# Conditioned residual block, 16 x 512 tokens: the hand-listed order of head, window and last group is listed anew

## The chip, the cores and the metric

The kernel runs on one core of one Trainium2 chip. Time is device time of one launch in microseconds (us). A core has five engines with an instruction queue each: PE (TensorE, matrix products into PSUM), DVE (VectorE), ACT (ScalarE), POOL (GpSimd) and SP (SyncE, which here only issues transfers). Each engine takes its instructions strictly in order; between engines only semaphores hold. PSUM has eight banks of 128 x 512 f32; PE writes there, DVE and ACT read it, POOL works on SBUF alone.

## The reference

For every token (row x of 512 numbers) six branches are made, weighted, joined to 3072 numbers and sent through a two-layer network with a layer norm; the result is added to x.

```python
h = _ln(x, pw_g[pathway_ids], pw_b[pathway_ids])
h = _ln(h, cp_g[compartment_ids], cp_b[compartment_ids])
t = _ln(x, tm_g[time_steps], tm_b[time_steps])
m = x + _mlp_ln(memory_state, ...)[:, None, :]     # n, r alike
s = _ln(x, ms_g[scale_type], ms_b[scale_type])
cat = jnp.concatenate([w[0] * h, w[1] * t, w[2] * m, w[3] * n, w[4] * r, w[5] * s], axis=-1)
return x + _mlp_ln(cat, int_W1, int_b1, int_W2, int_b2, int_g, int_be)
```

There are 16 x 512 = 8192 tokens, `_mlp_ln` is silu between two products and a layer norm behind them, and everything is f32.

## The kernel before, in words

Tokens are sorted by their (compartment, scale type) group and taken in 16 windows of 512, a window being four blocks of 128 rows. The first layer is computed from three operands, each turned so that its 512 columns lie on partitions: X (x itself, for the branches m, n, r), V (x normed, for t and s) and H (the twice normed branch h). V has weights of its own for each block of 128, built on the spot by `s_part` and `build`.

All work is cut into small pieces with two-letter names, and three texts list them: ORDER (line 20: set-up, windows 0 and 1, the start of 2), WINDOW (line 53) and LAST (line 69, the last window). `run` (line 1213) goes through such a text and calls each piece's function, which records its instructions. Nothing is reordered afterwards: every engine gets its instructions in the order of the list, and the waits follow from the data. WINDOW is run for windows 0 to 14 and leaves out what has been done already. In a name such as `rd.c.1.4` the letter is the window in relation to the current one: `o` two before, `p` one before, `c` the current one, `n` the next, `m` the one after; the digits are blocks or pairs of blocks.

Windows 2 to 14 compute the X and H share of layer 1 with seven products of half blocks instead of eight, for each of two pairs p of blocks. That is where GpSimd's sums come in. The pieces that matter here:

| pieces | engine | what they do |
|---|---|---|
| `p7.w.p.k`, `vp.w.g.n` | PE | one half-block product of X and H (L407), of V (L416): 22 in a window |
| `l2.w.j` | PE | layer 2 of one block (L351) |
| `rd.w.p.i` | DVE | adds one half bank of PSUM to the SBUF tile `add` (L427): 22 in a window |
| `la` | DVE | reads layer 2 from PSUM, adds a row (L458) |
| `tv`, `tx`, `th`, `tz` | DVE | 32 x 32 transposes of V, X, H and of the hidden layer (L186) |
| `f1`, `f2`, `bd`, `lb` | DVE | work on two or three SBUF operands: pathway affine (L288, L289), compartment (L312), the four chunks of `build` (L231), the last norm (L484, L485) |
| `hv`, `xe`, `xm`, `lv` | DVE | small statistics |
| `ss.w.p.0` to `ss.w.p.3` | POOL | the four sums of X and H blocks for the seven products (L377, L381, L383, L385) |
| `sh.w.j` | POOL | adds a row to the x block (L320) |
| `wq`, `wr` | POOL | sums of the weights, before the first and after the last of these windows (L353 to L366) |
| `gx`, `gh`, `gc`, `ga`, `po` | POOL | gathers of x, pathway rows, compartment rows and layer-1 rows (L160), the scatter of the result (L489) |
| `xp`, `fp`, `lp` | POOL | inverse roots (L253, L304, L476) |
| `xs`, `hb`, `nv`, `xn`, `fn`, `sp`, `hs`, `lq` | ACT | sums, norms, the first half of the V weights (L225), silu, squares |
| `sX`, `sV`, `sH`, `sZ` | SP | the transfers that complete a transposition (L194) |

What can hold a POOL sum is data alone: `ss.w.p.0` needs the X rows landed, `ss.w.p.1` the H rows, `ss.w.p.2` and `ss.w.p.3` the end of the products that read the old values; `sh` needs only that the window's norms have been read. The seven products accumulate within a bank, so that a product can wait for a read (`rd`) of what stands there, and a read for a product.

Of the kernel before, what the change touches and what calls it, by code (L numbers as in the profile page):

```python
# [18 lines left out]

ORDER = """  # L20
    sz scl bx lt ax wk.1.3 h2.1 wk.1.0 ac lw wk.1.1 se xt.0.0 by h2.2 pwi dk lh sp.0.0 gh.0.1 gh.0.0 xt.0.1 kd
    bd.0.0 cv he.1 xv.0.1 xv.0.0 dp px tt gh.0.2 xs.0.0 wk.1.2 wk.2.3 tk xs.0.1 h2.0 pk xs.0.2 gx.e0.2 xs.0.3 eh.1
    wk.2.0 he.2 cg xe.0 he.0 gx.e0.1 wh xp.0 xt.0.2 eh.0 gx.e0.0 xm.0 dc wk.2.1 xn.0.0 eh.2 cs xt.0.3 nv.0.0 cp
    xv.0.3 wk.2.2 cn gc.0.0 tb tv.0.0 xv.0.2 ct gx.e0.3 lo xs.e0.2 xa xn.0.1 do xs.e0.0 gr.e0.0 ca lX.0.2 xs.e0.1
    f1.0.0 nv.0.1 nv.0.3 cm xs.e0.3 nv.0.2 gr.e0.2 hb.0.0 f1.0.1 xe.e0 gx.e1.3 tv.0.3 gx.e1.0 wm tv.0.2 tv.0.1
    lX.0.3 gx.e1.1 cr xp.e0 gc.0.1 xm.e0 nv.e0.0 sV.0.2 nv.e0.2 f2.0.0 xn.0.2 hb.0.1 mt.e0.0 nv.e0.3 nv.e0.1 tr.e0.0
    sV.0.3 sV.0.0 mt.e0.2 gx.e1.2 tr.e0.2 lX.0.0 f2.0.1 lX.0.1 gr.e0.3 sp.0.1 gr.e0.1 hv.0.1 xs.e1.2 mt.e0.3 gx.1.1
    gr.e1.1 fp.0.1 sV.0.1 gc.0.2 tr.e0.3 mt.e0.1 xs.e1.1 rp.1 tr.e0.1 gr.e1.3 gc.0.3 fn.0.1 bd.0.1 sE.e0.1 sE.e0.0
    xs.e1.3 xs.e1.0 f1.0.2 gh.0.3 xn.0.3 lV.0.0 gx.1.2 hb.0.2 rp.0 hv.0.0 sE.e0.2 lV.0.1 th.0.1 rc.0 xe.e1 f1.0.3
    f2.0.2 xp.e1 fp.0.0 hv.0.2 xm.e1 hb.0.3 gx.1.0 hv.0.3 gc.1.0 fp.0.2 rc.1 tx.1.1 ex.1 fn.0.0 fp.0.3 ex.0 sE.e0.3  # L30
    f2.0.3 nv.e1.1 fn.0.3 th.0.0 tx.1.0 ro.0 fn.0.2 gx.1.3 th.0.3 gh.1.3 sp.0.2 xs.1.3 xs.1.0 ro.1 nv.e1.0 th.0.2
    xs.1.2 sH.0.0 bd.0.2 xs.1.1 mt.e1.1 tr.e1.1 sH.0.2 ex.2 ea.0 ex.3 sp.0.3 tx.1.3 gr.e1.0 ee.0 gx.2.1 mt.e1.0
    tr.e1.0 gc.1.3 nv.e1.3 lV.0.2 eo.0 tx.1.2 xe.1 xp.1 nv.e1.2 gr.e1.2 gh.1.0 bd.0.3 ea.1 sh.0.2 xm.1 lH.0.0 ea.2
    gx.2.3 xs.2.1 mt.e1.2 nv.1.0 sH.0.1 lH.0.2 mt.e1.3 sX.1.1 xn.1.0 gh.1.2 lH.0.1 xn.1.3 ea.3 tr.e1.2 tr.e1.3 ea.4
    tv.1.0 sX.1.0 f1.1.3 sh.0.1 gx.2.0 gx.2.2 lV.0.3 xn.1.2 gc.2.0 f1.1.0 gc.1.2 ee.1 ee.2 hb.1.3 hv.1.3 sE.e1.0
    hb.1.0 lX.1.0 f2.1.3 nv.1.1 f1.1.2 ex.4 f2.1.0 sE.e1.1 wl.1 ex.5 ea.6 sH.0.3 eo.2 fp.1.3 sE.e1.2 nv.1.2 lH.0.3
    sp.1.1 ea.5 hv.1.0 fp.1.0 ee.3 nv.1.3 sh.0.3 ee.4 hb.1.2 ex.6 bd.1.1 xs.2.3 fn.1.0 gh.1.1 gc.1.1 ar eo.3 fn.1.3
    tv.1.1 wl.3 tv.1.3 f2.1.2 hv.1.2 th.1.0 fp.1.2 eo.4 tv.1.2 xn.1.1 gh.2.1 xs.2.0 sX.1.2 xs.2.2 ee.5 th.1.3 sX.1.3
    eo.1 wl.2 ee.6 eo.5 xe.2 f1.1.1 eo.6 xp.2 tx.2.0 sp.1.0 lX.1.2 lX.1.3 sh.1.2 fn.1.2 xm.2 hb.1.1 tx.2.3 tx.2.1
    bd.1.0 ga.0.0 ha.0.0 nv.2.2 sV.1.0 ga.0.2 hv.1.1 ga.0.3 f2.1.1 fp.1.1 wl.0 ha.0.2 sh.1.0 th.1.2 hs.0.0 ga.0.1  # L40
    fn.1.1 sh.1.3 th.1.1 hs.0.2 xn.2.1 f1.2.1 gc.2.1 wl.4 sh.1.1 gh.2.3 lX.1.1 lV.1.0 sp.1.2 sV.1.2 sh.0.0 ha.0.3
    hs.0.3 bd.1.2 sV.1.1 ha.0.1 lV.1.1 ga.1.2 sp.1.3 tx.2.2 xn.2.0 sV.1.3 gh.2.0 sH.1.0 tz.0.0 tv.2.2 ga.1.0 hs.0.1
    tz.0.2 wq.3 hb.2.1 sH.1.3 tz.0.1 lV.1.2 nv.2.1 bd.1.3 tz.0.3 wq.1 lH.1.0 lV.1.3 lH.1.3 f2.2.1 nv.2.0 sp.2.1
    tv.2.0 nv.2.3 sp.2.0 bd.2.1 ga.1.3 bd.2.0 f1.2.0 wq.2 xn.2.3 sH.1.2 sX.2.1 sH.1.1 hv.2.1 sZ.0.3 hb.2.0 fp.2.1
    tv.2.3 wq.0 ha.1.0 tv.2.1 fn.2.1 f2.2.0 hv.2.0 l2.0.3 sZ.0.1 sh.2.3 fp.2.0 ga.2.2 la.0.3 ha.1.3 l2.0.1 sZ.0.2
    la.0.1 sX.2.2 ga.2.0 lq.0.1 l2.0.2 hs.1.0 fn.2.0 sZ.0.0 sV.2.1 l2.0.0 sV.2.2 hs.1.3 ga.1.1 tz.1.0 sX.2.0 xn.2.2
    sV.2.0 la.0.2 lq.0.2 th.2.0 tz.1.3 la.0.0 lq.0.0 th.2.1 lq.0.3 lH.1.2 lv.0 lH.1.1 ha.1.2 sV.2.3 gh.2.2 hs.1.2
    lp.0 sX.2.3 gh.3.1 lb.0.1 lb.0.0 gx.3.1 gx.3.0 ha.1.1 po.0.1 hs.1.1 lb.0.3 gx.3.3 tz.1.2 xs.3.1 tz.1.1 ga.2.3
    po.0.0 lb.0.2 gx.3.2 xs.3.0 ga.2.1 po.0.2
"""  # L50
# [1236 lines left out]
```

## Time and profile before

| | us |
|---|---|
| three timed runs, median (lowest, highest) | 1129.79 (1126.06, 1133.42) |
| the profiled execution, as timed | 1131.24 |
| its span in the profile | 1129.5 |
| the head, up to the first product of window 2 | 210.1 |
| windows 2 to 14, from one first product to the next | 62.3 to 65.0 |
| the last group, from the last first product | 974.4 to 1129.5 |

The mean clock that TensorE was granted is 0.95. In the profile's lines an engine's name stands ahead of the line of the kernel (L231) and the operation; then come output and input by the program's names, the shape, and how many. Busy time of an engine is what its instructions took; idle time before an instruction is put down to what released it. POOL's share of DMA instructions is the time of their issue, not of the transfer.

The costliest groups of DVE and POOL that the change reorders, in the same execution:

| group | instructions | mean ns |
|---|---|---|
| L231 `build` | 252 | 952 |
| L289, second half of `f1` | 64 | 1213 |
| L312 `f2` | 64 | 1113 |
| L484, first half of `lb` | 56 | 1250 |
| L485, second half of `lb` | 56 | 897 |
| L186, transposes of H | 64 | 680 |
| L458 `la` | 64 | 671 |
| L377, L381, L383, L385 `ss` | 26 each | 1279, 1354, 1282, 1463 |

### The profile page before, as it was taken

How to read it: one execution, taken by the hardware profiler on the slowest of the kernel's cores; microseconds unless marked ns; L12 is line 12 of the kernel's file. 1: busy time of each engine (PE TensorE's matmuls, PEld its weight loads, DVE VectorE, ACT ScalarE, POOL GpSimd, SP SyncE). 2: the span in 40 equal slices, each digit the busy share in tenths (PEclk: the TensorE clock that was granted, in tenths of full speed). 3: DMA queues.
4: the chain of work that ended last, by engine and by line, in shares of the span. 5: the costliest groups of instructions: out<-in, count | busy, mean ns of one | idle time of the engine just before them, and what ended most of it. 6: DMA issues, size and time to landing. Idle time of an engine off the chain costs nothing. (4 is left out here: it accounts for less than half of the span.)

```text
span 1129.5 us, 13393 instructions
## 1 busy us (share of the span) xinstructions
PE 986.7 (87%) x3577; PEld 652.2 (58%) x3577; DVE 920.4 (81%) x1466; ACT 656.2 (58%) x1432; POOL 712.8 (63%) x702
## 2 busy tenths in 40 slices
...
GB/s 296 238 155 222 248 214 177 220 126 191 169 144 176 142 222 127 200 122 190 168 145 201 128 212 132 187 129 180 180 140 187 143 214 130 192 126 136 112 51 93
DMA packets 91895, 191.07 MB, mean 169 GB/s; under 512 B 25364, under 2 KB 25364, under 8 KB 91820
## 3 DMA queue, kind: packets, MB, share of 16 engines
...
q14 instruction: 46, 0.38, 0.1%
...
## 5 line engine op out<-in xcount | busy, mean ns | idle before, releaser
L351 PE MATMUL p<-w,cZ 128*128 128x512 f32 x512 | 225.9, 595 | 10.1 <-DMA cZ<-rZ 7.1
L231 DVE SCALAR_TENSOR_TENSOR vs<-wt,sct,vs 128x512 f32<-128x512 f32 x252 | 225.1, 952 | 0.0
L225 ACT ACTIVATE vs<-ws,scs 128x512 f32<-128x512 f32 x252 | 160.8, 708 | 23.6 <-PE pqv L416 21.2
L351 PEld LDWEIGHTS p<-w,cZ 128*128 128x128 f32 x512 | 95.4, 190 | 133.6 <-issue 132.0
L489 POOL DMA_INDIRECT out<-yb,tok x64 | 69.2, 1082 | 106.8 <-DVE yb L454 39.3
L294 ACT ACTIVATE junk<-pw 128x512 bf16<-128x512 f32 x64 | 40.2, 629 | 162.8 <-issue 100.9
L160 POOL DMA_INDIRECT pw<-in_pw,i_pw x64 | 63.9, 999 | 83.0 <-issue 51.1
L339 ACT ACTIVATE add<-add 128x512 f32<-128x512 f32 x64 | 38.9, 626 | 120.1 <-DVE add L427 79.6
L416 PE MATMUL pqv<-vs,cV 128*128 128x256 f32 x416 | 107.5, 398 | 0.4 <-DVE vs L231 0.4
L160 POOL DMA_INDIRECT xbs<-in_x,tok x64 | 71.2, 1113 | 51.3 <-DVE yb L485 30.8
L312 DVE SCALAR_TENSOR_TENSOR pw<-pw,mvh,cp 128x512 f32<-128x512 f32 x64 | 71.2, 1113 | 27.0 <-DMA cp<-cp_rows,i_cp 26.4
L416 PEld LDWEIGHTS pqv<-vs,cV 128*128 128x128 f32 x416 | 81.4, 200 | 19.6 <-DVE vs L231 7.9
L320 POOL TENSOR_TENSOR xbs<-xbs,rows 128x512 f32<-128x512 f32 x64 | 81.3, 1271 | 0.4
L160 POOL DMA_INDIRECT cp<-cp_rows,i_cp x64 | 66.5, 1039 | 22.9 <-issue 10.4
L160 POOL DMA_INDIRECT add<-rows,i_add x64 | 62.9, 983 | 26.6 <-issue 14.5
L289 DVE TENSOR_TENSOR pw<-pw 128x512 f32<-128x512 f32 x64 | 77.6, 1213 | 2.2
L308 ACT ACTIVATE pw<-pw,rsh 128x512 f32<-128x512 f32 x64 | 44.0, 711 | 51.5 <-DVE pw L312 45.1
L484 DVE SCALAR_TENSOR_TENSOR yb<-yb,rsy,rows 128x512 f32<-128x512 f32 x56 | 70.0, 1250 | 1.0 <-POOL rsy L476 1.0
L243 ACT ACTIVATE junk<-xbs 128x512 bf16<-128x512 f32 x72 | 44.8, 623 | 33.3 <-DMA xbs<-in_x,tok 31.9
L407 PE MATMUL pq_0b<-wh__80,cH 128*128 128x256 f32 x104 | 35.4, 500 | 27.8 <-DVE add L427 16.1
L381 POOL TENSOR_TENSOR cX<-cX,cH 128x512 f32<-128x512 f32 x26 | 35.2, 1354 | 36.3 <-DMA cH<-rH 33.6
L463 ACT ACTIVATE junk<-yb 128x512 bf16<-128x512 f32 x64 | 40.3, 630 | 28.2 <-DVE yb L458 26.4
...
## 6 DMA issues: line engine op xcount, KB each, us to landing
cV<-rV SPq DMA_DIRECT2D x256, 64.0 KB
cH<-rH SPq DMA_DIRECT2D x256, 64.0 KB
cZ<-rZ SPq DMA_DIRECT2D x256, 64.0 KB
...
```

The lines of the kernel that those rows point to most:

```text
L160: nc.gpsimd.indirect_dma_start(dst, None, table, bass.IndirectOffsetOnAxis(ap=idx, axis=0), **kw)
L225: nc.scalar.activation(v[:, c], ws[:, c], AF.Identity, scale=scs[:, c, g, w : w + 1])
L231: nc.vector.scalar_tensor_tensor(v[:, c], wt[:, c], sct[:, c, g, w : w + 1], v[:, c], ALU.mult, ALU.add)
L243: nc.scalar.activation(junk, x, AF.Identity, accum_out=sums[:, 0, j : j + 1])
L289: nc.vector.tensor_add(pw[:, :D], pw[:, :D], pw[:, D:])
L308: nc.scalar.mul(pw[:, :D], pw[:, :D], st.pop(("rs", j)))
L312: nc.vector.scalar_tensor_tensor(pw[:, :D], pw[:, :D], st["mv", j][:, 1:2], cp, ALU.add, ALU.mult)
L320: nc.gpsimd.tensor_add(st["xb"][:, j, :], st["xb"][:, j, :], rows[:, 2, :])
L351: nc.tensor.matmul(p2, st["cZ"][:, j, c, :], w2[:, c, :], start=(c == 0), stop=(c == NC - 1))
L416: nc.tensor.matmul(home, st["cV"][:, g, c], st["v", g][:, c, n * H : (n + 1) * H], start=(b == 0 and n == 1 and c == 0), stop=(c == NC - 1 ...
L484: nc.vector.scalar_tensor_tensor(y, y, st["rsy"][:, j : j + 1], rows[:, 1, :], ALU.mult, ALU.mult)
L489: nc.gpsimd.indirect_dma_start(out_rows, bass.IndirectOffsetOnAxis(ap=tok[:, j, w : w + 1], axis=0), yb[:, j, :], None)
```

## The change

The three lists hold the same pieces as before in another order. No function changes, no piece is added or left out, no size or buffer changes. What moves in WINDOW, beside many smaller things: the list is cut at another place, so that `vp.c.0.1` is now its first product; `bd.c.2` moves from behind the layer-2 products to the window's start; `ss.c.1.0` to the very start, `ss.c.0.0` behind `xp.n`; only one layer-2 product (`l2.p.1`) now stands between the first products and `p7.c.0.7`, and the other three are spread over the following ones; `sh.c.1` moves from late in the list to the middle; the sums `ss.c.0.1`, `ss.c.1.1`, `ss.c.1.2` stand one behind another. In LAST, the weight sums `wr.0` to `wr.2` come first and `e1` (the first use of the square root) later.

```diff
 WINDOW = """
-    gc.c.3 f1.c.3 p7.c.0.1 vp.c.0.0 xs.n.3 f1.c.2 sZ.p.1 gc.c.2 hb.c.3 xs.n.2 xe.n xp.n hb.c.2 po.o.3 xm.n vp.c.0.1
-    rd.c.0.0 sZ.p.0 p7.c.1.1 hv.c.3 vp.c.1.1 sZ.p.2 l2.p.1 ss.c.0.0 hv.c.2 sp.c.2 fp.c.3 la.p.1 nv.n.3 fp.c.2 xn.n.1
-    f2.c.2 sh.c.0 tv.n.3 nv.n.1 f2.c.3 sZ.p.3 tv.n.1 gc.n.1 gh.n.0 l2.p.0 la.p.0 ss.c.1.0 fn.c.3 th.c.3 l2.p.2
-    l2.p.3 fn.c.2 th.c.2 sH.c.3 f1.n.1 la.p.3 la.p.2 p7.c.0.7 nv.n.2 tv.n.2 rd.c.0.1 p7.c.1.7 sH.c.1 hb.n.1 hv.n.1
-    lq.p.3 vp.c.1.0 sh.c.2 lq.p.1 bd.c.2 rd.c.1.0 vp.c.2.1 lq.p.2 lq.p.0 rd.c.1.1 ss.c.1.1 sp.c.3 lv.p lp.p bd.c.3
-    tx.n.1 nv.n.0 gc.n.0 sH.c.2 p7.c.1.5 vp.c.3.0 ss.c.1.2 sH.c.0 xn.n.2 tv.n.0 f2.n.1 xn.n.0 lb.p.3 lb.p.0 tx.n.0
-    vp.c.3.1 sp.n.1 sV.n.3 rd.c.1.2 f1.n.0 rd.c.0.10 rd.c.0.9 hb.n.0 vp.c.2.0 fp.n.1 p7.c.0.2 lb.p.2 gh.n.3 ss.c.0.1
-    tx.n.2 sV.n.1 po.p.0 fn.n.1 gx.m.0 sV.n.0 sp.n.0 sV.n.2 lb.p.1 p7.c.1.2 tx.n.3 sX.n.0 ss.c.0.2 hv.n.0 ss.c.0.3
-    gx.m.1 ss.c.1.3 p7.c.0.5 rd.c.0.2 bd.n.0 gx.m.3 xn.n.3 rd.c.1.9 p7.c.1.6 rd.c.1.6 sX.n.2 p7.c.0.6 fp.n.0
-    rd.c.0.4 rd.c.1.3 p7.c.0.3 sh.c.1 sX.n.1 gx.m.2 xs.m.0 xs.m.1 gh.n.2 rd.c.0.5 rd.c.1.10 p7.c.1.3 po.p.1 rd.c.0.3
-    rd.c.1.7 ga.n.1 rd.c.1.5 th.n.1 rd.c.0.6 p7.c.0.4 rd.c.0.8 ga.n.2 hs.c.2 tz.c.2 sX.n.3 po.p.2 hs.c.1 p7.c.1.4
-    rd.c.0.7 rd.c.1.8 gh.m.1 ga.n.0 rd.c.1.4 ga.n.3 hs.c.3 f2.n.0 hs.c.0 tz.c.1 tz.c.3 tz.c.0 sh.n.3 fn.n.0 th.n.0
-    bd.n.1
+    vp.c.0.1 p7.c.0.1 vp.c.0.0 sp.c.2 ss.c.1.0 vp.c.1.1 sZ.p.1 bd.c.2 p7.c.1.1 gc.c.3 xs.n.2 f1.c.3 sZ.p.2 vp.c.2.0
+    vp.c.2.1 f1.c.2 p7.c.1.7 gc.c.2 xs.n.3 xe.n xp.n rd.c.0.10 xm.n rd.c.0.9 l2.p.1 ss.c.0.0 hb.c.3 hv.c.3 hb.c.2
+    fp.c.3 nv.n.0 hv.c.2 fp.c.2 sZ.p.3 f2.c.3 fn.c.3 f2.c.2 p7.c.0.7 sZ.p.0 l2.p.2 sh.c.0 fn.c.2 rd.c.0.1 th.c.2
+    gh.n.0 nv.n.1 th.c.3 xn.n.1 vp.c.1.0 sp.c.3 l2.p.0 tv.n.1 la.p.1 nv.n.2 tx.n.0 nv.n.3 f1.n.1 tx.n.2 bd.c.3
+    rd.c.1.1 sH.c.1 l2.p.3 sH.c.3 vp.c.3.0 sH.c.2 lq.p.1 sh.c.2 rd.c.0.0 tv.n.2 gc.n.0 gc.n.1 la.p.0 rd.c.1.9 po.o.3
+    rd.c.1.0 la.p.2 sh.c.1 tv.n.3 lq.p.0 ss.c.0.1 ss.c.1.1 ss.c.1.2 tx.n.1 p7.c.1.5 la.p.3 vp.c.3.1 sH.c.0 p7.c.0.2
+    hb.n.1 f2.n.1 gh.n.3 lq.p.2 ss.c.0.2 tv.n.0 lq.p.3 lv.p p7.c.0.5 xn.n.0 sV.n.3 hv.n.1 sV.n.2 sV.n.1 f1.n.0
+    sV.n.0 lp.p tx.n.3 xn.n.2 lb.p.1 fp.n.1 fn.n.1 th.n.1 rd.c.1.10 rd.c.1.2 rd.c.0.6 lb.p.0 hb.n.0 p7.c.1.4
+    ss.c.0.3 lb.p.3 p7.c.1.2 lb.p.2 gx.m.1 sp.n.1 sp.n.0 gh.m.1 p7.c.1.6 f2.n.0 hv.n.0 xn.n.3 gx.m.0 rd.c.1.8
+    rd.c.0.2 po.p.0 rd.c.1.6 fp.n.0 rd.c.1.4 rd.c.1.5 p7.c.0.6 hs.c.3 p7.c.0.4 ss.c.1.3 p7.c.1.3 gx.m.2 tz.c.3
+    rd.c.0.5 rd.c.0.4 fn.n.0 sh.n.3 rd.c.0.8 xs.m.1 gx.m.3 sX.n.0 rd.c.0.3 bd.n.0 rd.c.1.3 rd.c.1.7 hs.c.1 hs.c.2
+    po.p.1 ga.n.0 p7.c.0.3 ga.n.1 ga.n.2 rd.c.0.7 hs.c.0 th.n.0 gh.n.2 tz.c.2 sX.n.3 po.p.2 sX.n.2 xs.m.0 tz.c.0
+    ga.n.3 sX.n.1 tz.c.1 bd.n.1
 """
 LAST = """
-    sp.c.2 e0 f1.c.2 gc.c.2 f1.c.3 lV.c.0 hb.c.2 hv.c.2 hb.c.3 sZ.p.1 gc.c.3 hv.c.3 lV.c.1 l2.p.1 sZ.p.2 l2.p.2
-    po.o.3 f2.c.2 e1 fp.c.3 la.p.1 sh.c.2 wr.2 sp.c.3 bd.c.2 la.p.2 lq.p.1 wr.1 f2.c.3 sZ.p.0 wr.0 lq.p.2 fp.c.2
+    wr.0 wr.1 sp.c.2 wr.2 lV.c.0 bd.c.2 lV.c.1 sp.c.3 sZ.p.1 f1.c.3 e0 sZ.p.0 f1.c.2 sZ.p.2 lV.c.2 wr.3 bd.c.3
+    hb.c.2 lX.c.2 gc.c.2 lX.c.1 hv.c.2 gc.c.3 hb.c.3 f2.c.2 fp.c.2 sZ.p.3 f2.c.3 hv.c.3 fn.c.2 th.c.2 fp.c.3 l2.p.0
...
```

ORDER is listed anew in the same way from its third line on (`pk`, `xa`, `wm` later, `wk` and the front of window 0 in another order); up to `h2.0` it is as before.

68 lines of the change are left out of this document (34 added, 34 removed).

## The prediction
> **What bounds the kernel now.** I read the page first, then the timeline of TensorE, VectorE and GpSimd over one steady window, then the busy time by stretches.
>
> ```profile
> span 1129.5 us, 13393 instructions
> ...
> PE 986.7 (87%) x3577; PEld 652.2 (58%) x3577; DVE 920.4 (81%) x1466; ACT 656.2 (58%) x1432; POOL 712.8 (63%) x702
> ```
>
> No engine is full, so the waits between them decide. TensorE's timeline (start, length, instructions, in brackets what ended the idle time before):
>
> ```profile
> 210.13 1.89 PE L407 MATMUL pq_0a<-wx__79,cX 128*128 128x256 f32 x8
> ...
> 592.79 1.89 PE L407 MATMUL pq_0a<-wx__79,cX 128*128 128x256 f32 x8
> 594.52 1.89 PE L416 MATMUL pq_0a<-vs,cV 128*128 128x256 f32 x8
> ...
> 601.43 7.09 PE L351 MATMUL p<-w,cZ 128*128 128x512 f32 x16
> ...
> 619.34 1.99 PE L407 MATMUL pq_1b<-wxt,s 128*128 128x256 f32 x8 [1.60 <-POOL s L377]
> 623.24 2.78 PE L416 MATMUL pq_0b<-vs,cV 128*128 128x256 f32 x8 [1.91 <-DVE add L427]
> ...
> 646.11 1.97 PE L407 MATMUL pq_0b<-wh__80,cH 128*128 128x256 f32 x8 [1.92 <-DVE add L427]
> ...
> 654.32 3.13 PE L407 MATMUL pq_1b<-wxt,cH 128*128 128x256 f32 x8 [2.79 <-DVE add L427]
> ...
> 974.39 1.89 PE L407 MATMUL pq_0a<-wx__79,cX 128*128 128x256 f32 x8
> ```
>
> Each window of 512 tokens begins with the pq_0a product: twelve windows lie between 210.13 and 974.39, so one takes 63.7 us. TensorE's own work in it is 22 products of 1.73 us (592.79 to 594.52) and four layer-2 products of 3.5 (7.09 for two): 52.0. The rest is four waits, 8.2 us in this window, three of them for VectorE's reads of PSUM (L427), and products at half speed behind a wait (2.78 and 3.13 instead of 1.89). So I ask what makes VectorE late.
>
> ```profile
> 613.31 1.65 DVE L312 SCALAR_TENSOR_TENSOR pw<-pw,mvh,cp 128x512 f32<-128x512 f32 x1
> ...
> 617.97 3.09 DVE L289 TENSOR_TENSOR pw<-pw 128x512 f32<-128x512 f32 x1
> 620.98 1.27 DVE L458 TENSOR_TENSOR yb<-p,rows 128x512 f32<-128x512 f32 x2
> 622.18 0.69 DVE L186 STREAM_TRANSPOSE rV<-xm 128x512 f32<-128x512 f32 x1
> 622.80 0.38 DVE L427 TENSOR_TENSOR add<-pq_0b,add 128x256 f32<-128x256 f32 x1
> ...
> 623.17 3.51 DVE L231 SCALAR_TENSOR_TENSOR vs<-wt,sct,vs 128x512 f32<-128x512 f32 x4
> ...
> 627.33 2.73 DVE L231 SCALAR_TENSOR_TENSOR vs<-wt,sct,vs 128x512 f32<-128x512 f32 x4
> ...
> 632.07 0.74 DVE L484 SCALAR_TENSOR_TENSOR yb<-yb,rsy,rows 128x512 f32<-128x512 f32 x1
> 632.85 0.69 DVE L485 TENSOR_TENSOR yb<-yb,xbs 128x512 f32<-128x512 f32 x1
> 633.46 2.18 DVE L484 SCALAR_TENSOR_TENSOR yb<-yb,rsy,rows 128x512 f32<-128x512 f32 x1
> ...
> 639.20 2.12 DVE L484 SCALAR_TENSOR_TENSOR yb<-yb,rsy,rows 128x512 f32<-128x512 f32 x1
> 641.35 1.65 DVE L485 TENSOR_TENSOR yb<-yb,xbs 128x512 f32<-128x512 f32 x1
> ...
> 645.88 5.73 DVE L231 SCALAR_TENSOR_TENSOR vs<-wt,sct,vs 128x512 f32<-128x512 f32 x4
> 651.53 0.41 DVE L427 TENSOR_TENSOR add<-pqv,add 128x256 f32<-128x256 f32 x1
> 651.87 0.41 DVE L427 TENSOR_TENSOR add<-pq_1a,add 128x256 f32<-128x256 f32 x1
> ```
>
> ```profile
> 618.01 1.27 POOL L377 TENSOR_TENSOR s<-cX 128x512 f32<-128x512 f32 x1
> 619.23 1.27 POOL L320 TENSOR_TENSOR xbs<-xbs,rows 128x512 f32<-128x512 f32 x1
> ...
> 633.79 1.29 POOL L381 TENSOR_TENSOR cX<-cX,cH 128x512 f32<-128x512 f32 x1
> ...
> 639.48 1.27 POOL L383 TENSOR_TENSOR cX<-cX 128x512 f32<-128x512 f32 x1
> 640.83 1.61 POOL L385 TENSOR_TENSOR cH<-cH,cX 128x512 f32<-128x512 f32 x1
> ...
> 655.97 0.96 POOL L160 DMA_INDIRECT pw<-in_pw,i_pw  x1 [3.48 <-issue]
> 657.24 1.01 POOL L489 DMA_INDIRECT out<-yb,tok  x1 [0.30 <-issue]
> ```
>
> The same instruction takes 0.69 or 0.74 us, or 1.6 to 3.1: the long ones lie under GpSimd's sums of 1.27. L289 at 617.97 spans two sums and ends 0.56 after the second. Only VectorE's two-operand work on SBUF does this; the L458 reads of PSUM (1.27 for two) and the transposes do not lengthen. Excess over the free length, row by row: 0.91 (613.31), 2.40 (617.97), 0.78 (623.17), 1.44 (633.46), 1.38 (639.20), 0.96 (641.35), 3.00 (645.88): **10.9 us a window**, about 1.25 a sum. And it lies where VectorE has nothing to give:
>
> ```profile
> 612.70:657.50 44.80, 36.58 (x145) 28.94 (x144) 43.88 (x65) 23.95 (x50) 28.32 (x25) 0.93 0.49 131
> ```
>
> VectorE (the third busy time) is busy 43.88 of 44.80 us from 19.9 us into the window to its end. A stall there moves the window's end by its own length. From the page's groups, the sums of L320 (the last column is idle time before them, in all):
>
> ```profile
> L320 POOL TENSOR_TENSOR xbs<-xbs,rows 128x512 f32<-128x512 f32 x64 | 81.3, 1271 | 0.4
> ```
>
> All 64 together waited 0.4 us: nothing holds them until the moment at which the list has them.
>
> The Trainium skill ("SBUF — State Buffer", Who interferes with whom) says that a VectorE instruction with two SBUF inputs contends with a GpSimd one that reads SBUF, and that whichever issues first holds the shared pair while the other blocks. The trace agrees on who collides, not on the winner: L484 began at 633.46, the sum 0.33 later, yet the sum kept its 1.29 and L484 paid; at 640.83 the sum did wait (1.61).
>
> **The change, part by part.** No instruction is added or taken away; each engine gets its own in another order, and GpSimd is still held by nothing but data. So I go through the new WINDOW by hand, counting from TensorE's first product in it, and place each sum by GpSimd's own queue: 1.27 for a sum, 1.27 from one gather to the next (655.97 to 657.24).
>
> First part, to p7.c.0.7. Ahead of its end stand nine products and one layer-2 product: 9 x 1.73 + 3.5 = 19.1, and 1.2 for one product at half speed (3.13 against 1.89), 20.3. VectorE has less to do here (four transposes, two builds of L231, two front_1, two front_less): some 12 of 20 us. The sums ss.c.1.0, ss.c.0.0 and sh.c.0 fall here; ss.c.1.0 meets bd.c.2, as the add gathers before it wait for the last tz. That costs nothing on the path while VectorE waits anyway for rd.c.0.1, which TensorE releases at 20.3; without that cover each would cost 1.27.
>
> Second part, rd.c.0.1 to rd.c.1.7, which frees the bank that the next window's first product (vp.n.0.1) takes. VectorE has 19 reads at 0.34 (651.53 to 651.87), 12 transposes at 0.62 (622.18 to 622.80), four L458 at 0.60, 22 two-operand instructions at 0.68 (2.73 for four) and some small ones: 6.5 + 7.4 + 2.4 + 15.0 + 0.2 = 31.5, and I leave 1.2 for bd.c.3, which waits for ScalarE's sp.c.3, and tz.c.3, which waits for hs.c.3. That is 53.0 for a window without a stall.
>
> Nine sums remain. sh.c.2 follows gh.n.0, which th.c.2 frees: it meets transposes and la.p.1, nothing. Then GpSimd runs ahead of the list: gc.n.0, gc.n.1 and po.o.3 wait for nothing of this window, so sh.c.1 comes some 6 us after th.c.2 instead of beside rd.c.1.0, and meets bd.c.3; ss.c.0.1 and ss.c.1.1 stand right behind. Two to three collisions, 3.3. ss.c.1.2 and ss.c.0.2 then meet reads, la and transposes: nothing. ss.c.0.3 waits for p7.c.0.2 and fp.n.1 and meets lb.p.1 or lb.p.0: 1.25. ss.c.1.3 stands behind fp.n.0 and meets reads and tz.c.3: nothing for VectorE, though p7.c.1.3 waits 1 to 3 us for it, covered by bd.n.0 and the last reads. sh.n.3 meets the first piece of bd.n.0: 0.7. Sum 5.3, between 2.6 (two sums) and 8.9 (seven of nine at 1.27).
>
> TensorE in this part: p7.c.1.4 waits for rd.c.1.2, a read of the same bank, at about 44; seven products, 12.1, follow it and end at 56, still ahead of VectorE.
>
> Window: 53.0 + 5.3 = 58.3, against 63.7. The other way round, 10.9 - 5.3 = 5.6, less 0.4 because the full stretch begins at 20.3 and not 19.9, gives 5.2; I take 5.3. There are 13 such windows (numbers 2 to 14): **69 us**. By the page's rule of the first to issue, half of these collisions would be GpSimd's and the 5.3 would be some 2.7.
>
> Head and tail:
>
> ```profile
> 80.00:210.00 130.00, 117.16 (x261) 49.49 (x260) 99.88 (x162) 93.62 (x198) 88.13 (x88) 0.97 0.72 206
> 1038.00:1067.60 29.60, 21.85 (x43) 8.43 (x42) 22.18 (x31) 15.21 (x32) 19.38 (x19) 0.83 0.47 144
> 1067.60:1119.50 51.90, 51.87 (x121) 22.73 (x119) 22.03 (x37) 9.34 (x20) 8.52 (x8) 1.00 0.24 66
> ```
>
> In the head TensorE (first busy time) is idle 12.8 of 130 us, in the start of the last group 7.8 of 29.6; from 1067.6 on it is full and the new LAST can bring nothing before the end. Head: between 12.8 gained and 6 lost, since a full relisting may open new waits as well as close them; I take 3. Tail: wr.0 to wr.2 move ahead of bd.c.2, which frees lV.c.2 of the collisions but may put them on bd.c.2 itself; between 7.8 gained and 4 lost, 3 taken.
>
> Sum: 69 + 3 + 3 = 75. The profiled execution took 1131.24 us as timed, 1129.5 of it the span: 1131.2 - 75 = 1056. The median of the runs is 1.4 lower, well inside the spread of 1126 to 1133, so I leave **1056**.
>
> **The rivals.**
>
> *The plan holds better than my hand count.* If gathers keep GpSimd back so that sums stand where the list has them, or if an operation that has begun keeps its operands (the page's rule), stalls are about 2.7: 2.6 x 13 = 34 more, 1022. For it: 640.83, where the sum waited. Against: the 0.4 us of L320, sums run ahead. 0.15.
>
> *The change does not do what it says.* Sums run ahead everywhere, and seven of nine still meet two-operand work: 8.9 of stalls, windows of 61.9, 13 x 1.8 + 6 = 29, that is 1102. For it: about 15 of the 31.5 us in the second part are two-operand work, so blind placing hits about six of nine. Against: the old list does worse than blind (10.9 / 1.25, nearly nine hits of twelve), so the orders do matter. 0.15.
>
> *Slower: TensorE waits for ss.c.0.0.* In the old list four layer-2 products stand between the window's first products and p7.c.0.7; in the new one a single one. ss.c.0.0 stands on GpSimd behind ga.n.3, ss.c.1.0, two gathers and xp.n, which waits for xe.n, behind f1.c.2, which waits for the gather gh.n.2 that is issued only between the last tz. By my count the sum ends 2 us before it is needed (some 15.4 against 8 x 1.73 + 3.5 = 17.3). This kind of wait exists today (1.60 at 619.34). Each us beyond those 2 adds one to the window; the window is as long as now when the sum is 2 + 5.3 = 7.3 late, and at 9.5 late the kernel takes 1131 + 13 x 2.2 - 6 = 1154. That needs a gather that lands some 8 us after its use. 0.11.
>
> **How the numbers follow.** The forecast has 0.59: 1056, alone between 1035 and 1085 (stalls from 3.7 to 7.5, head and tail from both bounds). The range reaches to the better case and the one with seven hits: 1016 to 1106; outside are the slow rival and the edges. A change of 1% (11 us) is about what this measurement tells from none. Faster by over 1%: the forecast, the better case and half of the seven-hits case and more, 0.83; within 1%: 0.06; slower: 0.11.
>
> **What would show it.** Windows of about 58 us between pq_0a products. L289, L484 and L485 near 0.7 us; L231 still long once per window, under sh.c.1. TensorE's waits for L427 shorter in sum than 6.6. The step is wrong if L320's sums begin beside reads of PSUM (better) or if VectorE's excess stays above 8 (seven hits); the slow rival shows as a wait of several us for s (L377) ahead of pq_0b<-wxt,s.

## The result, and the profile after

| | before | after |
|---|---|---|
| median of four runs, us | 1129.61 (1126.06 to 1133.42) | 1021.37 (1020.52 to 1026.26) |
| ratio, 95% interval | | 0.9052 (0.9017 to 0.9087) |
| profiled execution as timed / its span | 1131.24 / 1129.5 | 1026.26 / 1024.2 |
| first product of window 2 | 210.1 | 206.6 |
| twelve periods from there, mean | 63.7 | 56.8 |
| from the last first product to the end | 155.1 | 136.3 |

The profiled executions lie 105.0 us apart as timed, 105.3 by their spans: 3.5 in the head, 12 x 6.9 = 83 in the steady part and 18.8 behind it, of which 6.9 is put down to the thirteenth window and 11.9 to the last group. The first of the twelve periods took 66.8 us in the changed kernel, with a pause of ScalarE in it that is shown below; the other eleven took 55.9 in the mean, against 63.6 before. The page of the changed kernel, span and busy time of each engine:

```profile
span 1024.2 us, 13367 instructions
...
PE 945.6 (92%) x3577; PEld 643.4 (63%) x3577; DVE 848.8 (83%) x1466; ACT 655.4 (64%) x1432; POOL 703.5 (69%) x702
```

VectorE does the same 1466 instructions in 71.6 us less, TensorE its own in 41 less: instructions got shorter. The groups of VectorE's two-operand work (count, busy time, mean ns of one) show where; their means before were 952, 1213, 1113, 1250 and 897:

```profile
L231 DVE SCALAR_TENSOR_TENSOR vs<-wt,sct,vs 128x512 f32<-128x512 f32 x252 | 215.9, 924 | 10.3 <-ACT vs L225 10.3
L289 DVE TENSOR_TENSOR pw<-pw 128x512 f32<-128x512 f32 x64 | 55.2, 863 | 2.2
L312 DVE SCALAR_TENSOR_TENSOR pw<-pw,mvh,cp 128x512 f32<-128x512 f32 x64 | 50.8, 799 | 7.9 <-DMA cp<-cp_rows,i_cp 6.9 <-ACT junk L296 0.7
...
L484 DVE SCALAR_TENSOR_TENSOR yb<-yb,rsy,rows 128x512 f32<-128x512 f32 x56 | 47.0, 839 | 1.2 <-POOL rsy L476 1.2
L485 DVE TENSOR_TENSOR yb<-yb,xbs 128x512 f32<-128x512 f32 x56 | 40.8, 729 | 1.9
```

One window as VectorE has it (start, length, what ended the idle time before):

```profile
783.27 1.64 DVE L289 TENSOR_TENSOR pw<-pw 128x512 f32<-128x512 f32 x1
...
791.15 1.75 DVE L312 SCALAR_TENSOR_TENSOR pw<-pw,mvh,cp 128x512 f32<-128x512 f32 x1 [0.44 <-DMA cp<-cp_rows,i_cp]
792.84 0.42 DVE L427 TENSOR_TENSOR add<-pq_0b,add 128x256 f32<-128x256 f32 x1
...
796.76 0.87 DVE L288 TENSOR_TENSOR pw<-xn,pw 128x512 f32<-128x512 f32 x1
...
800.86 3.38 DVE L231 SCALAR_TENSOR_TENSOR vs<-wt,sct,vs 128x512 f32<-128x512 f32 x1
...
812.96 1.14 DVE L484 SCALAR_TENSOR_TENSOR yb<-yb,rsy,rows 128x512 f32<-128x512 f32 x1
814.13 0.69 DVE L485 TENSOR_TENSOR yb<-yb,xbs 128x512 f32<-128x512 f32 x1
...
823.44 1.09 DVE L427 TENSOR_TENSOR add<-pq_1a,add 128x256 f32<-128x256 f32 x3 [1.35 <-PE pq_1a L407]
```

And GpSimd's sums in it:

```profile
782.84 1.52 POOL L377 TENSOR_TENSOR s<-cX 128x512 f32<-128x512 f32 x1
...
791.09 1.27 POOL L320 TENSOR_TENSOR xbs<-xbs,rows 128x512 f32<-128x512 f32 x1
...
801.19 1.27 POOL L320 TENSOR_TENSOR xbs<-xbs,rows 128x512 f32<-128x512 f32 x1
802.41 1.27 POOL L381 TENSOR_TENSOR cX<-cX,cH 128x512 f32<-128x512 f32 x1
...
812.10 1.45 POOL L385 TENSOR_TENSOR cH<-cH,cX 128x512 f32<-128x512 f32 x1
...
824.53 1.28 POOL L320 TENSOR_TENSOR xbs<-xbs,rows 128x512 f32<-128x512 f32 x1
```

The excess over the free lengths is 0.95 (783.27) and 1.01 (791.15) ahead of the read at 792.84, and behind it 0.18, 2.64 (800.86, under sh.c.1 and ss.c.0.1 back to back) and 0.40: 5.2 in place of 10.9. TensorE in the same window:

```profile
773.53 1.89 PE L416 MATMUL pqv<-vs,cV 128*128 128x256 f32 x8
...
787.48 3.60 PE L351 MATMUL p<-w,cZ 128*128 128x512 f32 x8
790.91 1.89 PE L407 MATMUL pq_0b<-wxt,s 128*128 128x256 f32 x8
...
816.27 2.52 PE L407 MATMUL pq_1b<-wxt,cH 128*128 128x256 f32 x8 [2.74 <-DVE add L427]
818.58 3.09 PE L407 MATMUL pq_1a<-wh__80,cH 128*128 128x256 f32 x8
...
830.15 1.89 PE L416 MATMUL pqv<-vs,cV 128*128 128x256 f32 x8
```

From vp.c.0.1 (773.53) to the next one (830.15) the window takes 56.6 us, and one wait is left, with two slow products behind it (2.52 and 3.09 us in place of 1.89; the granted clock is 0.67 from 816.27 to 821.50, and 1.00 behind that).

### The profile page after: what moved, and what is told of

Read it like the earlier page. It is cut to its first block, busy times and chain, and to the rows that moved or that the text cites. A ratio compares the mean times of both kernels' runs of the same rounds, so it can differ in the third digit from the quotient of the medians.

```text
span 1024.2 us, 13367 instructions
## 1 busy us (share of the span) xinstructions
PE 945.6 (92%) x3577; PEld 643.4 (63%) x3577; DVE 848.8 (83%) x1466; ACT 655.4 (64%) x1432; POOL 703.5 (69%) x702
## 4 chain that ended last, share of the span: by engine, by line
PE 37%; DVE 24%; issue 10%; DMA 9%; POOL 7%; SPq 6%; ACT 4%; another core or an unknown queue 2%; DVEq 0%; POOLq 0%; ACTq 0%
PE p L351 11%; DVE vs L231 6%; PE p L332 5%; SPq L194 5%; PE pq_1b L407 4%; PE pqv L416 4%; PE pq_1a L407 3%; PE pq_0b L407 3%; DVE add L427 3%; DMA cV<-rV 2%; DMA cp<-cp_rows,i_cp 2%; PE pq_0a L407 2%; DVE rX L186 2%; DVE yb L458 2%
## 5 line engine op out<-in xcount | busy, mean ns | idle before, releaser
L351 PE MATMUL p<-w,cZ 128*128 128x512 f32 x512 | 228.8, 596 | 2.2 <-ACT junk L294 2.2
L231 DVE SCALAR_TENSOR_TENSOR vs<-wt,sct,vs 128x512 f32<-128x512 f32 x252 | 215.9, 924 | 10.3 <-ACT vs L225 10.3
L351 PEld LDWEIGHTS p<-w,cZ 128*128 128x128 f32 x512 | 97.7, 191 | 109.7 <-issue 106.5
L489 POOL DMA_INDIRECT out<-yb,tok x64 | 70.1, 1096 | 55.9 <-DVE yb L454 21.1
L416 PE MATMUL pqv<-vs,cV 128*128 128x256 f32 x416 | 101.2, 385 | 0.0
L160 POOL DMA_INDIRECT add<-rows,i_add x64 | 66.8, 1044 | 49.6 <-DVE rZ L186 34.3
L160 POOL DMA_INDIRECT pw<-in_pw,i_pw x64 | 63.2, 987 | 36.7 <-DVE rH L186 19.9
L416 PEld LDWEIGHTS pqv<-vs,cV 128*128 128x128 f32 x416 | 78.7, 192 | 14.8 <-issue 3.8
L160 POOL DMA_INDIRECT cp<-cp_rows,i_cp x64 | 69.9, 1092 | 22.5 <-issue 14.3
L288 DVE TENSOR_TENSOR pw<-xn,pw 128x512 f32<-128x512 f32 x64 | 48.6, 760 | 26.6 <-DMA pw<-in_pw,i_pw 12.8
L308 ACT ACTIVATE pw<-pw,rsh 128x512 f32<-128x512 f32 x64 | 45.7, 718 | 29.3 <-POOL rsh L304 19.3
L407 PE MATMUL pq_1b<-wxt,cH 128*128 128x256 f32 x104 | 32.3, 465 | 31.3 <-DVE add L427 24.3
L304 POOL TENSOR_TENSOR rsh<-veh,mhalf 128x1 f32<-128x1 f32 x64 | 41.8, 658 | 22.8 <-DVE veh L300 17.8
L312 DVE SCALAR_TENSOR_TENSOR pw<-pw,mvh,cp 128x512 f32<-128x512 f32 x64 | 50.8, 799 | 7.9 <-DMA cp<-cp_rows,i_cp 6.9
L289 DVE TENSOR_TENSOR pw<-pw 128x512 f32<-128x512 f32 x64 | 55.2, 863 | 2.2
L265 ACT ACTIVATE xm<-xbs,nmx,rsx 128x512 f32<-128x512 f32 x64 | 50.2, 803 | 9.4 <-DVE nmx L261 7.8
```

Source lines behind the costliest of these rows:

```text
L160: nc.gpsimd.indirect_dma_start(dst, None, table, bass.IndirectOffsetOnAxis(ap=idx, axis=0), **kw)
L231: nc.vector.scalar_tensor_tensor(v[:, c], wt[:, c], sct[:, c, g, w : w + 1], v[:, c], ALU.mult, ALU.add)
L289: nc.vector.tensor_add(pw[:, :D], pw[:, :D], pw[:, D:])
L312: nc.vector.scalar_tensor_tensor(pw[:, :D], pw[:, :D], st["mv", j][:, 1:2], cp, ALU.add, ALU.mult)
L351: nc.tensor.matmul(p2, st["cZ"][:, j, c, :], w2[:, c, :], start=(c == 0), stop=(c == NC - 1))
L407: nc.tensor.matmul(home, m[:, c], at_["half"][k][:, c], start=(c == 0 and k in (1, 7)), stop=(c == NC - 1), skip_group_check=True)
```

## The experiments

The first question: is it the collisions, or the rest of the relisting? The sums of GpSimd are cut to 8 of their 512 columns in both kernels, and the rest of them is left out; the order and the waits are kept.

```diff
-        nc.gpsimd.tensor_add(st["xb"][:, j, :], st["xb"][:, j, :], rows[:, 2, :])
+        nc.gpsimd.tensor_add(st["xb"][:, j, :8], st["xb"][:, j, :8], rows[:, 2, :8])
...
-        a11, a12, a21, a22, _ = t
+        a11, a12, a21, a22, _ = [m[:, :8] for m in t]
```

> The kernel before with each of GpSimd's sums (xb + rows, L320, and the operand sums of the X and H products, L377 to L385) on 8 of its 512 columns: the rest of these sums is left out, the order of every engine and all waits stay. Theory A (sums that meet VectorE's two-operand work cost the time): the 10.9 us of VectorE's excess go from each window, which then takes 53 to 56 us in place of 63.7, the kernel 990 to 1030 us; L289, L312, L484 and L485 are near 0.7 us everywhere. Rival B (the rest of the order, which the sums' size leaves alone, makes the difference between the two lists): windows stay above 61 us, the kernel above 1100.

> The same cut in the changed kernel: each of GpSimd's sums on 8 of its 512 columns, the rest of these sums left out, the order kept. Theory A: VectorE's excess of 4 to 5 us a window goes, of which 2 to 4.5 come through since TensorE's 52 us are close: 52.3 to 54.8 us a window, the kernel 960 to 995 us; the two lists then differ by under 45 us in place of 108. Rival B: as the sums don't make the difference, the two lists still differ by 90 to 110 us.

Measured: 1030.74 us (ratio 0.9115, 0.9045 to 0.9184) and 968.08 (0.8594, 0.8565 to 0.8623). Both theories hold in part. The sums cost the list before 97 us and the new one 53, so the collisions matter; yet without them the lists still differ by 63, where A had under 45 and B 90 or more. VectorE's excess fell to some 1.2 us a window in the list before, 9.7 less, but its windows only from 63.7 to 56.6. The timeline of TensorE in that run, then that of SP's transfers:

```profile
603.93 1.89 PE L416 MATMUL pqv<-vs,cV 128*128 128x256 f32 x8
610.41 15.66 PE L351 MATMUL p<-w,cZ 128*128 128x512 f32 x32 [4.58 <-DMA cZ<-rZ]
```

```profile
591.88 11.00 SPq L194 DMA_DIRECT2D cX<-rX  x16
602.98 11.04 SPq L194 DMA_DIRECT2D cZ<-rZ  x16
```

The window's fifth product ends, and layer 2 (L351) waits 4.58 us for cZ, whose 16 transfers queue behind the 16 of cX. VectorE has the last transpose of rZ done at 600.58; the first transfer of cZ starts 2.4 us later, right behind cX, and the product 7.4 us after that. TensorE's waits for cZ are 36.0 us in all in this run. That is a second limit. In the kernel before, TensorE's waits (us in all, times, the longest) show only the edge of it:

```profile
PE p L351 <- DMA cZ<-rZ: 7.1, 10, 1.3
```

The new list with small sums has 0.7 us of this wait in all: from 679.38 to 731.20 a window takes 51.8 us, which is TensorE's own work:

```profile
679.38 1.89 PE L407 MATMUL pq_0a<-wx__79,cX 128*128 128x256 f32 x8
...
731.20 1.89 PE L407 MATMUL pq_0a<-wx__79,cX 128*128 128x256 f32 x8
```

So the second limit was tried by itself: in the new list the first layer-2 product goes back to stand behind five products, with full and with small sums.

```diff
-    vp.c.0.1 p7.c.0.1 vp.c.0.0 sp.c.2 ss.c.1.0 vp.c.1.1 sZ.p.1 bd.c.2 p7.c.1.1 gc.c.3 xs.n.2 f1.c.3 sZ.p.2 vp.c.2.0
-    vp.c.2.1 f1.c.2 p7.c.1.7 gc.c.2 xs.n.3 xe.n xp.n rd.c.0.10 xm.n rd.c.0.9 l2.p.1 ss.c.0.0 hb.c.3 hv.c.3 hb.c.2
+    vp.c.0.1 p7.c.0.1 vp.c.0.0 sp.c.2 ss.c.1.0 vp.c.1.1 sZ.p.1 bd.c.2 p7.c.1.1 sZ.p.2 l2.p.1 gc.c.3 xs.n.2 f1.c.3 vp.c.2.0
+    vp.c.2.1 f1.c.2 p7.c.1.7 gc.c.2 xs.n.3 xe.n xp.n rd.c.0.10 xm.n rd.c.0.9 ss.c.0.0 hb.c.3 hv.c.3 hb.c.2
```

> The changed kernel with the first layer-2 product (l2.p.1) and its transfer's place moved ahead to stand behind five products, as in the list before, in place of eight; all sums as in the changed kernel. Theory C (the old list had a second limit behind the collisions: layer 2 stood too early for the transfer of cZ, which in the run with small sums and the old list held TensorE 35 us): the transfer lands some 4.7 us after 778.7, the product would start at 782.3, so TensorE waits 1 to 3 us with what half speed adds, in 13 windows: 1035 to 1060 us. Rival: VectorE, which bounds the window, takes no notice: 1016 to 1026 us.

> The changed kernel with the same move of l2.p.1 and with GpSimd's sums on 8 of 512 columns (the rest of these sums left out). Theory C: here TensorE is full, so each wait for cZ comes through: 13 times 1.2 to 3 us on 968, 984 to 1007 us, with TensorE's waits for cZ in the trace. Rival: the transfer is there in time, 965 to 972 us.

Measured: 1072.53 (0.9550, 0.9511 to 0.9589) and 1031.25 (0.9184, 0.9146 to 0.9221): theory C, at a higher price than expected. With full sums, TensorE's waits for cZ (us in all, times, the longest), then TensorE and SP:

```profile
PE p L351 <- DMA cZ<-rZ: 50.0, 13, 5.0
```

```profile
686.20 1.89 PE L407 MATMUL pq_1a<-wx__79,cX 128*128 128x256 f32 x8
691.77 5.37 PE L351 MATMUL p<-w,cZ 128*128 128x512 f32 x8 [3.68 <-DMA cZ<-rZ]
```

```profile
674.16 10.07 SPq L194 DMA_DIRECT2D cX<-rX  x16
684.33 11.56 SPq L194 DMA_DIRECT2D cZ<-rZ  x16
```

The product starts 7.4 us after the first transfer of cZ, not 4.7, and then runs at 5.37 in place of 3.60. The 4.7 came from the kernel before, where the first transfer of cZ (596.71) did not stand right behind cX; that cX is what makes the difference is not shown. VectorE's stalls are those of the changed kernel: 922, 861 and 800 ns in the mean for L231, L289 and L312. The four runs and the two kernels make a table (medians, us):

| list | all sums | sums on 8 columns |
|---|---|---|
| before | 1129.6 | 1030.7 |
| new, l2.p.1 behind five products | 1072.5 | 1031.2 |
| new | 1021.4 | 968.1 |

Read down the second column: without collisions, layer 2's place alone is worth 63 us, and the rest of the relisting nothing that these runs can tell (ratios 0.9115 and 0.9184, with intervals that overlap). Down the first: the rest is worth 57 (there are fewer collisions) and layer 2's place another 51; by the ratios, each to the kernel before timed beside it, 51 and 56. So each is about half of the gain.

Whether GpSimd's being busy or its reading of two operands holds VectorE: in the list before, an instruction with one input beside each small sum, the subtractions that make s excepted.

```diff
+        nc.gpsimd.tensor_scalar(own, own, 1.0, None, ALU.mult)
```

> The kernel before with GpSimd's sums on 8 of 512 columns (the rest of these sums left out), and behind each of those that were full, the subtractions that make s excepted, a GpSimd instruction with one input, 384 columns of a tile of its own multiplied by 1. So GpSimd is kept about as busy as before, with one operand in place of two. Theory A in its narrow form (only GpSimd's work with two inputs holds VectorE's two-operand work): VectorE's excess stays near 1 us a window and the time near that with small sums, 1022 to 1045 us. Rival (any of GpSimd's work on SBUF holds it, or its time alone counts): an excess of 5 us and more a window, 1075 to 1125 us.

Measured: 1039.01 (0.9243, 0.9191 to 0.9296), the narrow form. GpSimd, then VectorE at the same time:

```profile
654.76 1.21 POOL L379 TENSOR_SCALAR own<-own 128x384 f32<-128x384 f32 x1
...
656.61 1.16 POOL L379 TENSOR_SCALAR own<-own 128x384 f32<-128x384 f32 x1
```

```profile
655.09 0.75 DVE L484 SCALAR_TENSOR_TENSOR yb<-yb,rsy,rows 128x512 f32<-128x512 f32 x1
655.88 0.69 DVE L485 TENSOR_TENSOR yb<-yb,xbs 128x512 f32<-128x512 f32 x1
```

L484 lies wholly under an instruction of 1.21 us and takes its free 0.75; under a sum it took 2.18 and 2.12 before. Where such an instruction begins inside one of VectorE's, VectorE's gets a little longer: L485 at 478.63 takes 0.87 in place of 0.69, and an L379 begins at 478.93. The Trainium skill ("SBUF — State Buffer", Who interferes with whom) has VectorE's two-input work contend with a GpSimd instruction that reads SBUF; for sums with two inputs the traces agree, for these with a single input they do so only in this small part.

The parts alone, in the kernel before: the new list for the steady part, then that for the last group.

> The kernel before with the new list for the steady part alone, the head's and the last group's lists as they were. Theory A, with the parts independent as the prediction had them: twelve windows 6.9 us shorter and one that the last list shares, 1035 to 1060 us (77 to 90 us gained, head and tail give the other 15 to 30). Rival B, with the gain from how the three lists fit each other: above 1075.

> The kernel before with the new list for the last group alone. The prediction gave it 3 us (1121 to 1127 against 1124 to 1130); the two traces, compared from the last group's first product to the end, 11.9 us: 1114 to 1120. With the head's list as before, what is left of the 108 us behind the steady part (77 to 95) and the tail is the head's.

Measured: 1033.76 (0.9175, 0.9142 to 0.9208), 94 us of the 108, and 1119.71 (0.9932, 0.9905 to 0.9958), 5.7 us, between the 3 of the prediction and the 11.9 that the two traces show behind the steady part. Of that 11.9 some 7 come without the new last list: with the new steady part alone the stretch from the last first product to the end takes 140.9 us, against 155.1 before and 136.3 with all three lists. The steady part carries the gain; some 8 us are left for the head and for what the parts do together.

Next the collisions by place. Two sums that cost nothing were moved to where VectorE has `lb`:

```diff
-    fp.c.3 nv.n.0 hv.c.2 fp.c.2 sZ.p.3 f2.c.3 fn.c.3 f2.c.2 p7.c.0.7 sZ.p.0 l2.p.2 sh.c.0 fn.c.2 rd.c.0.1 th.c.2
+    fp.c.3 nv.n.0 hv.c.2 fp.c.2 sZ.p.3 f2.c.3 fn.c.3 f2.c.2 p7.c.0.7 sZ.p.0 l2.p.2 fn.c.2 rd.c.0.1 th.c.2
...
-    rd.c.1.1 sH.c.1 l2.p.3 sH.c.3 vp.c.3.0 sH.c.2 lq.p.1 sh.c.2 rd.c.0.0 tv.n.2 gc.n.0 gc.n.1 la.p.0 rd.c.1.9 po.o.3
+    rd.c.1.1 sH.c.1 l2.p.3 sH.c.3 vp.c.3.0 sH.c.2 lq.p.1 rd.c.0.0 tv.n.2 gc.n.0 gc.n.1 la.p.0 rd.c.1.9 po.o.3
...
-    ss.c.0.3 lb.p.3 p7.c.1.2 lb.p.2 gx.m.1 sp.n.1 sp.n.0 gh.m.1 p7.c.1.6 f2.n.0 hv.n.0 xn.n.3 gx.m.0 rd.c.1.8
+    ss.c.0.3 lb.p.3 p7.c.1.2 lb.p.2 gx.m.1 sh.c.0 sh.c.2 sp.n.1 sp.n.0 gh.m.1 p7.c.1.6 f2.n.0 hv.n.0 xn.n.3 gx.m.0 rd.c.1.8
```

> The changed kernel with two sums that cost nothing there (sh.c.0 and sh.c.2, beside reads and transposes) moved behind gx.m.1, where VectorE has lb.p.3 and lb.p.2 (L484 and L485, two operands in SBUF); nothing else moved. Theory A: two collisions of 1.0 to 1.3 us more in each of 13 to 14 windows, 26 to 36 us: 1047 to 1058 us, with two of the L484 or L485 at 1.6 to 2.2 us in each window. Rival B: no change beyond 5 us from 1021.

Measured: 1028.39 (0.9127, 0.9097 to 0.9158), only 7 us more than the changed kernel. VectorE, then GpSimd:

```profile
798.77 2.15 DVE L231 SCALAR_TENSOR_TENSOR vs<-wt,sct,vs 128x512 f32<-128x512 f32 x1
...
815.90 2.77 DVE L484 SCALAR_TENSOR_TENSOR yb<-yb,rsy,rows 128x512 f32<-128x512 f32 x1
```

```profile
799.09 1.28 POOL L320 TENSOR_TENSOR xbs<-xbs,rows 128x512 f32<-128x512 f32 x1
801.79 1.59 POOL L381 TENSOR_TENSOR cX<-cX,cH 128x512 f32<-128x512 f32 x1 [1.42 <-DMA cH<-rH]
...
815.61 2.51 POOL L320 TENSOR_TENSOR xbs<-xbs,rows 128x512 f32<-128x512 f32 x2
```

The two sums did hit: L484 took 2.77, 2.0 more than free. But without them in front GpSimd came to sh.c.1 earlier and ss.c.0.1 now waited for its transfer (1.42), so `build` met one sum in place of two (2.15, not 3.38): 1.2 us came back. And the rest did not come through in full. The price of a collision is right; counting moved sums by it is not, since every later sum moves too.

The other way, sh.c.1 was taken from under `build`, to where GpSimd idles and VectorE transposes.

```diff
-    fp.c.3 nv.n.0 hv.c.2 fp.c.2 sZ.p.3 f2.c.3 fn.c.3 f2.c.2 p7.c.0.7 sZ.p.0 l2.p.2 sh.c.0 fn.c.2 rd.c.0.1 th.c.2
+    fp.c.3 nv.n.0 hv.c.2 fp.c.2 sZ.p.3 f2.c.3 fn.c.3 f2.c.2 p7.c.0.7 sZ.p.0 l2.p.2 sh.c.0 sh.c.1 fn.c.2 rd.c.0.1 th.c.2
...
-    rd.c.1.0 la.p.2 sh.c.1 tv.n.3 lq.p.0 ss.c.0.1 ss.c.1.1 ss.c.1.2 tx.n.1 p7.c.1.5 la.p.3 vp.c.3.1 sH.c.0 p7.c.0.2
+    rd.c.1.0 la.p.2 tv.n.3 lq.p.0 ss.c.0.1 ss.c.1.1 ss.c.1.2 tx.n.1 p7.c.1.5 la.p.3 vp.c.3.1 sH.c.0 p7.c.0.2
```

> The changed kernel with one sum moved: sh.c.1 right behind sh.c.0, where GpSimd idles until th.c.2 and VectorE has a read and transposes; it no longer stands ahead of ss.c.0.1 under bd.c.3 (L231, 3.38 in place of 0.74). Theory A: ss.c.0.1 then comes only when its transfer of cH has landed, after bd.c.3; VectorE's excess falls from 4.7 to 1.5 to 3 us a window, 13 windows: 987 to 1010 us. Rival B (the stall is hidden or comes back elsewhere, as with the two sums moved back, where 1.7 us more of it made windows 0.7 longer): 1010 to 1021 us. Rival: ss.c.0.1 simply takes the free place under bd.c.3: one collision less, 1.3 us, 1004 us or more.

Measured: 988.67 (0.8792, 0.8764 to 0.8819), faster than both kernels, 33 us under the changed one (29 by the ratios). VectorE and GpSimd there:

```profile
596.70 2.35 DVE L288 TENSOR_TENSOR pw<-xn,pw 128x512 f32<-128x512 f32 x1
...
602.27 2.16 DVE L231 SCALAR_TENSOR_TENSOR vs<-wt,sct,vs 128x512 f32<-128x512 f32 x1
```

```profile
591.02 2.96 POOL L320 TENSOR_TENSOR xbs<-xbs,rows 128x512 f32<-128x512 f32 x2
...
597.20 1.30 POOL L320 TENSOR_TENSOR xbs<-xbs,rows 128x512 f32<-128x512 f32 x1
...
602.60 1.28 POOL L381 TENSOR_TENSOR cX<-cX,cH 128x512 f32<-128x512 f32 x1
```

ss.c.0.1 did take the free place under `build`, as the last rival had it, so one collision went, not two, and in some windows sh.c.2 now meets L288. The time lies where theory A had it, but not for its reason. Windows, from the second on, take 54.3 us in place of 55.9, some 19 us in twelve of them: one collision's worth, and the rest of the 33 us is not the collision (see the runs that follow).

Three more tried to go on from there: TensorE's wait for rd.c.1.2 (the 2.74 above) filled with two other products, sh.c.2 moved as well, and both moves without the products. The move of sh.c.1 is as above in all three.

```diff
-    rd.c.1.1 sH.c.1 l2.p.3 sH.c.3 vp.c.3.0 sH.c.2 lq.p.1 sh.c.2 rd.c.0.0 tv.n.2 gc.n.0 gc.n.1 la.p.0 rd.c.1.9 po.o.3
+    rd.c.1.1 sH.c.1 l2.p.3 sH.c.3 vp.c.3.0 sH.c.2 lq.p.1 rd.c.0.0 tv.n.2 gc.n.0 gc.n.1 la.p.0 rd.c.1.9 po.o.3
...
-    sV.n.0 lp.p tx.n.3 xn.n.2 lb.p.1 fp.n.1 fn.n.1 th.n.1 rd.c.1.10 rd.c.1.2 rd.c.0.6 lb.p.0 hb.n.0 p7.c.1.4
-    ss.c.0.3 lb.p.3 p7.c.1.2 lb.p.2 gx.m.1 sp.n.1 sp.n.0 gh.m.1 p7.c.1.6 f2.n.0 hv.n.0 xn.n.3 gx.m.0 rd.c.1.8
-    rd.c.0.2 po.p.0 rd.c.1.6 fp.n.0 rd.c.1.4 rd.c.1.5 p7.c.0.6 hs.c.3 p7.c.0.4 ss.c.1.3 p7.c.1.3 gx.m.2 tz.c.3
+    sV.n.0 lp.p tx.n.3 xn.n.2 lb.p.1 fp.n.1 fn.n.1 th.n.1 rd.c.1.10 rd.c.1.2 rd.c.0.6 lb.p.0 hb.n.0 p7.c.1.2 p7.c.1.6 p7.c.1.4
+    ss.c.0.3 lb.p.3 lb.p.2 gx.m.1 sp.n.1 sp.n.0 gh.m.1 f2.n.0 hv.n.0 xn.n.3 gx.m.0 rd.c.1.8
+    rd.c.0.2 po.p.0 rd.c.1.6 fp.n.0 rd.c.1.4 rd.c.1.5 p7.c.0.6 hs.c.3 p7.c.0.4 ss.c.1.3 p7.c.1.3 sh.c.2 gx.m.2 tz.c.3
```

> The changed kernel with sh.c.1 behind sh.c.0, as in the run before, and on TensorE p7.c.1.2 and p7.c.1.6, which wait for no read that late, ahead of p7.c.1.4, which waits 2.8 us for rd.c.1.2 and then runs at half speed. If that wait is on the path in the windows that TensorE still sets: 0 to 2.7 us from each of 13 windows, 955 to 985 us, I take 972. If VectorE alone sets them: 985 to 992.

> The run before it with sh.c.2 also moved, behind ss.c.1.3, where VectorE has reads of PSUM; it no longer stands under f1.n.1 (L288, 2.36 in place of 0.69). Theory A: 1 to 1.7 us less excess a window, 5 to 20 us less than that run. Rival: sh.n.3 comes 1.3 us later by it and falls on bd.n.0, which VectorE has last in the window: no gain, or up to 10 us more.

> The changed kernel with sh.c.1 behind sh.c.0 and sh.c.2 behind ss.c.1.3; TensorE's products in the order of the changed kernel. The two runs with p7.c.1.2 and p7.c.1.6 ahead took 999 us where the one without took 989, though their windows were equal in the profiles (54.3 and 54.5); they differ in the first window, which begins with a wait of 7.8 us of TensorE for VectorE's build L231 in the profiles of those two and without one in that of the 989. If the order of the products costs the 11 us: 980 to 991 us. If it was that wait, which any of these kernels can have: 985 to 1000, and the wait at the first window decides.

Measured: 999.63 (0.8862, 0.8826 to 0.8898), 999.09 (0.8854, 0.8827 to 0.8882) and 999.10 (0.8842, 0.8809 to 0.8875): none gains; they lie some 10 us above sh.c.1 moved alone, 6 to 8 by the ratios, and the interval of the third overlaps with its (0.8764 to 0.8819). The waits of TensorE (us in all, times, the longest), with sh.c.1 moved and then with the products too:

```profile
PE pq_1b L407 <- DVE add L427: 23.6, 12, 2.9
```

```profile
PE pq_0b L407 <- DVE add L427: 15.7, 13, 1.9
PE pq_1a L416 <- DVE vs L231: 7.8, 1, 7.8
```

The wait for a read became shorter at another bank, and windows stayed at 54.5 us (54.3 with sh.c.1 alone, both from the second on): that wait did not set them. That VectorE alone sets them, as the rival had it, is not shown either: with sh.c.2 moved too, L288 takes 683 ns in the mean in place of 816 and L312 858 in place of 924, and windows still take 54.5. The difference lies ahead of that: the second window begins at 248.4 us in the profile of sh.c.1 alone, and at 266.1, 268.3 and 269.1 in the others. Part of it is a single wait in the first window, the second row above. The changed kernel has it too, behind a pause of ScalarE:

```profile
219.74 2.56 ACT L225 ACTIVATE vs<-ws,scs 128x512 f32<-128x512 f32 x4 [9.48 <-remote]
```

The profiled run of sh.c.1 alone, at 980 us the fastest of its four (980 to 991), had no such pause, and its first window took 53.8 us where the changed kernel's took 66.8. The other three have the pause at the same place, 9.46, 9.19 and 7.59 us, the last with the products in the changed kernel's order, and first windows of 62.6 to 63.5. So some 9 us of their later start go with the pause and not with the order of the products. The rest, 9 to 12 us, lies in the head, whose list is the same in all four: the first product of window 2 comes at 194.6 us with sh.c.1 alone and at 203.6 to 206.4 in the others. What holds ScalarE there the trace gives as "remote" alone. Five of the fourteen profiles have the pause, all with the new list; four other profiles of that list do not. Why it comes, and how often it came in the runs without a profile, stays open.

## Why the prediction was right, and where not

**The time** lies in the range, 35 us under the forecast. Of the 30 between the two profiled differences (105 against 75) the windows make 13 x 1.6 = 21 and the tail 9 (11.9 against 3). That it lies in the range is partly luck: the sum had 69 us for collisions, where fewer collisions with all the rest brought 51 to 57, and nothing for layer 2's place, which brought 51 to 56.

**What bounds the kernel.** That GpSimd's sums lengthen VectorE's two-operand work is shown: small sums take the excess away and 97 us of the time, and one-input work in their place brings back 8 of them. That "Only VectorE's two-operand work on SBUF does this" goes too far: in the kernel before, L249 has one input of 128 x 4 and took 0.98 us at 604.98 and 1.53 at 732.14, each to the end of a sum that began at 604.64 and 732.35; it took 0.22 in the changed kernel at 786.77, with no sum beside it. And the two L458 at 620.98 do not show that reads of PSUM stay free, as they lie between two sums (one ends at 620.50, the next begins at 622.87); an L458 of the changed kernel does, 0.65 at 805.45 under the sum at 805.47. That "A stall there moves the window's end by its own length" held roughly for the new list (51.8 us a window without sums, 55.9 from the second window on with mostly 4.4 us of excess, part of it free) but not for the list before, where 9.7 us of excess were worth 7.1.

**The step that failed** is "the other way round, 10.9 - 5.3 = 5.6, less 0.4 because the full stretch begins at 20.3 and not 19.9": it takes the whole gain of a window out of the collisions, as if both lists had the same window without them. The count of the new window was near: 53.0 without a stall, 51.8 measured with small sums. But the 53.0 was counted along VectorE, and the 51.8 is TensorE's own work, so the run shows of VectorE's count only that it is no more than that. The list before has 56.6 there, because layer 2 waits for cZ. In the kernel before that wait hardly shows, since the stalls hid it; fewer collisions alone would have brought it up, as the run with l2.p.1 moved back shows. In the runs, layer 2's place, which enters the step only with 0.4 us for the later start of the full stretch, is worth 51 to 56 us of the 108, and the fewer collisions with all the rest 51 to 57. The prediction asked what is late next for VectorE's reads, and not for layer 2.

**First part**: p7.c.0.7 was put at 20.3 us into the window and ended at 792.80, 19.3; the product at half speed at the start did not occur. ss.c.1.0 met f1 (783.27) rather than bd.c.2, and sh.c.0 met f2 (791.15), both free as forecast: the read at 792.84 starts when the product ends.

**Second part**: 5.3 of stalls were forecast, 3.2 came in this window. The 3.3 at bd.c.3 came as 2.64, by sh.c.1 and ss.c.0.1 as named, while ss.c.1.1 waited for its transfer; the 1.25 at lb as 0.40; the 0.7 at bd.n.0 not at all, as sh.n.3 (824.53) ended before it. In other windows the excess was 3.3 to 8.0, mostly 4.4, first part included. That sums run ahead of the list was right.

**TensorE**: that p7.c.1.4 waits for rd.c.1.2 was right (816.27, 2.74), that VectorE stays behind it not quite: the products at half speed behind the wait (2.52 and 3.09) kept VectorE 1.35 us at 823.44.

**Head and tail**: 3 forecast for each; 3.5 and 11.9 measured. The head's agreement is chance: with the new head list and full sums, window 2 began at 194.6 to 206.6 us in seven profiles (210.1, 206.0 and 212.7 in three with the old one). The tail was mis-sized, and 5.7 when tried alone.

**The rivals**: "the plan holds better" (1022 us) came true in part. ss.c.1.1 and sh.n.3 were held back, and the second part's stalls, 3.2, lie nearer to its 2.7 than to 5.3. Its 1022 is the time that was measured, but by chance: it too has the time from collisions alone, and with the same stalls and l2.p.1 moved back the kernel takes 1072. The rule that it leaned on, that the first to issue keeps the operands (the Trainium skill, "SBUF — State Buffer", Who interferes with whom), the trace contradicts again: L231 at 800.86 began 0.33 ahead of the sum, and waited for it and for the next. Seven hits did not come. TensorE's waits for s are 0.8 us in the whole span, against 14.8 before.
